# First element of a graph network kernel: another order of its loads, biases as rows, y plus x on VectorE

## The chip, the cores and the metric

The kernel runs on one core of a Trainium2 chip. The metric is the device time of one execution in microseconds (us), a median over runs. A profiled execution gives the trace; its times are us from the start of its span unless marked ns. The engines are PE (TensorE, matmuls; PEld are its weight loads), DVE (VectorE), ACT (ScalarE), POOL (GpSimd) and SP (SyncE, which here only issues DMA transfers). ACT and POOL can issue transfers too.

## The reference

`x` is (16, 1024, 128), `adj` is (16, 1024, 1024), all in float32. A first graph layer is followed by a network of four layers with skip connections; each adds its input and normalises:

```python
# layer 0
degree = adj.sum(-1)[:, :, None]
agg = einsum('bid,bij->bjd', x, adj) / degree
x1 = layernorm(x + relu(concat([x, agg], -1) @ W.T + b))
# layer 1: four layers with inputs of 128, 128, 256 and 384 features
def layer(nodes, adj, ws, bs, wd, bd, wn, bn, wu, bu):
    src_agg = einsum('bjv,bij->biv', nodes @ ws + bs, l2norm(adj, 2))   # rows scaled
    dst_agg = einsum('bjv,bji->biv', nodes @ wd + bd, l2norm(adj, 1))   # columns scaled
    return tanh(concat([src_agg, nodes @ wn + bn, dst_agg], 2) @ wu + bu)
out = layernorm(x1 + four_layers(x1, adj))
```

## The kernel before

The 16 elements of the batch are worked off one after the other, and an element's preparation (loads, squares, norms, first graph layer) lies beside the products of the element before it. Element 0 has nothing before it, so its preparation is written out by hand ahead of the loop. The order on every engine is the order in which the program issues the instructions; pools of buffers and semaphores add waits, but nothing is reordered.

**Blocks.** `adj[0]` (4.2 MB) is held in the tile `a` as 8 blocks of 128 rows by 1024 columns. Two blocks are a row pair, and `PAIRS` lists the four pairs: the two of the second half of the nodes (h = 1) first, then those of h = 0. Each pair comes as four pieces, one for each group `g` of 32 partitions, each 256 KB. `x[0]` (0.5 MB) comes as four pieces of 64 KB a half into `xn`.

**Loads before.** SP issues `w0n` (the first layer's weights), then groups 0 and 1 of x of both halves, then groups 0 and 1 of all four row pairs. POOL issues the groups 2 and 3 of each. SP goes on with `b0c`, and then by layers with the weights and the four biases (`fetch_weights`; a bias is a column, one element of 4 bytes in each of 128 partitions), with row blocks of `adj` in another arrangement (`load_rows`, eight pieces of 128 KB for each of four quarters q) after layers 1, 2 and 3. The completions of SP's transfers use eight semaphores in turn, so a transfer is issued only when the eighth before it has landed. In the trace this is an SP issue that waits for a DMA.

**First graph layer.** `to_xT` transposes x on TensorE, with a copy on ACT. `weights_of_x` multiplies it by half of W into `pw`. `with_x` (L1168) multiplies the identity by x into a bank `pn`, to which y is added later. For each pair `squares_of` takes the squares of its two blocks with their sums on ACT (L1119) and the row sums (degrees) on VectorE (L1125), and `gathers_of` multiplies x by the blocks into `pa` (L1132, 128x512 each; a matmul in float32 shows as two instructions). `degree_inverses` and `degree_row` make 1/degree a row, by a reciprocal on VectorE, a transpose on TensorE (`dinv`, L359) and a copy on ACT. In block `second` = 3 the degree is taken on ACT (L1199). `scaled` is `pa` times that row (`agT`), `weights_of_agT` the second half of W, with the relu on ACT (`yT`, L1163). `with_y` (L1174) adds y to `pn` by products of yT with the identity. `norm_stats` takes mean and variance on VectorE, `norm_write_act` (ACT, L490) and `norm_write` (VectorE, L486) write x1 to `x1n`, and `to_x1` transposes it.

**Folding of weights.** A layer's ws, wd and wn are multiplied by wu ahead of use: `fold_begin` transposes them on TensorE (L205), copies them out (L206), and multiplies the biases by wu (L209, L211); `fold_end` multiplies the weights (L227) and copies them (L229, L230). Layers 0 and 1 are folded beside the normalisation. The folds of layers 2 and 3 stand in the loop over the products of layer 0 (`plain_layer`): before step i of its list of matmuls it calls `hooks[i]`, 5 and 8 for layer 2, 9 and 12 for layer 3. `small` hands out TensorE banks of a pool of two, `product` those of a pool of four.

**Layer 0 of element 0.** `messages` makes the messages in four groups of blocks, in the order 2, 3, 0, 1 (L247, `pt`), and calls `between[n]` after group n. After the third comes `row_factors0`: the inverse row norms are spread (L381), summed over groups on TensorE (`rp`, L252), copied (`rinv`), and two quarters of rows are scaled by them on ACT (L647). `plain_layer` then does the own products z, the destination products d (L851), and the source products z with the transposed rows (`at`, from VectorE's transposes, L655).

Of the kernel before, what the change touches and what calls it, by code (L numbers as in the profile page):

```python
# [8 lines left out]
F32 = mybir.dt.float32  # L9
# [14 lines left out]
def adj_resnorm_kernel(ctx: ExitStack, tc: tile.TileContext, x, adj, w0, b0, layers, out):  # L24
# [147 lines left out]
    def message_tile(name):  # L172

        return one.tile([P, max(WIDTH)], F32, tag="wm", name=name)
# [2 lines left out]

        return wm if l in PAIRED else wm[:, :KEPT[l] * 2 * P].rearrange("p (c v) -> p c v", v=2 * P)

    def fetch_weights(raw, l, q, wm=None):  # L180
        ws, bs, wd, bd, wn, bn, wu, bu = layers[l]
        nch = CHUNKS[l]
        size = max(3 * nch * P, KEPT[l] * 2 * P, WIDTH[l])
        flat = raw.take(size) if wm is None else wm[:, WIDTH[l]:]
        wr = flat[:, :3 * nch * P].rearrange("p (k c v) -> p k c v", k=3, c=nch)
        for k, w in enumerate((ws, wd, wn)):
            q.dma_start(wr[:, k], w.rearrange("(c p) v -> p c v", p=P))
        wur = raw.take(3 * P).rearrange("p (k v) -> p k v", k=3)
        q.dma_start(wur, wu.rearrange("(c p) v -> p c v", p=P))
        bc = raw.take(4)  # L190
        for k, v in enumerate((bs, bd, bn, bu)):
            q.dma_start(bc[:, k:k + 1], v.rearrange("(p o) -> p o", o=1))
# [48 lines left out]
    def small(name, shape=(K,)):  # L241
        return ps_s.tile([P, *shape], F32, tag="small", name=name)
# [811 lines left out]
    def load_pair(q, pair, groups):  # L1054
        h, k = pair
# [3 lines left out]
    def load_nodes(q, h, groups):  # L1059
        for g in groups:  # L1060
            q.dma_start(xn[g * C:(g + 1) * C, h * BPH:(h + 1) * BPH], xv[h][g])

    nc.sync.dma_start(w0n, w0)
    shares = ((nc.sync, range(G // 2)), (nc.gpsimd, range(G // 2, G)))
    for h in (1, 0):
        for q, groups in shares:
            load_nodes(q, h, groups)
    make_identity(nc, ident)
    for pair in PAIRS:
        for q, groups in shares:  # L1070
            load_pair(q, pair, groups)
    nc.sync.dma_start(b0c, b0.rearrange("(p o) -> p o", o=1))
    raw = Raw()
    wm = message_tile("wm1_0")
    Q = combined(0, "Q")
    places = {q: Q[i].rearrange("p k (u c) -> p (k u) c", u=2) for q, i in ((2, 2), (3, 3), (0, 4))}
    places[1] = one.tile([P, 2 * NJ, HW // 2], F32, tag="T2", name="rows1_0")
    rows, fetched = {}, []
    for l, q in enumerate((None, 2, 3, None)):
        fetched.append(fetch_weights(raw, l, nc.sync, None if l else wm))  # L1080
        if q is not None:
            rows[q] = load_rows(0, q, [places[q]])
    wm = as_chunks(wm, 0)
# [18 lines left out]
    pt = small("w0tr", [HW])  # L1102
    for k in range(2):
        nc.tensor.transpose(pt[:, k * P:(k + 1) * P], w0n[:, k * P:(k + 1) * P], ident)
    nc.scalar.copy(w0T.rearrange("p k v -> p (k v)"), pt[:, :2 * P])

    sq = []
    for p in (3, 4):
# [12 lines left out]
    def add_square(i):  # L1121
        nc.gpsimd.tensor_add(sq[4], sq[4], sq[i])
# [41 lines left out]

    def with_x(h):

        pn[h] = ps_t.tile([P, BPH, P], F32, tag="pt", name=f"yn0_{h}")
        nc.tensor.matmul(pn[h].rearrange("p q d -> p (q d)"), ident, xn[:, h * BPH:(h + 1) * BPH].rearrange("p q d -> p (q d)"),  # L1168
                         start=True, stop=False)

    def with_y(h):
        for q in range(BPH):
            i = h * BPH + q
            nc.tensor.matmul(pn[h][:, q], yT[:, i * P:(i + 1) * P], ident, start=False, stop=q == BPH - 1)  # L1174

    def to_x1(h):
        pt = product(f"x1tr_{h}")
# [8 lines left out]
    for pair in PAIRS[:2]:  # L1186
        squares_of(*pair)
        gathers_of(*pair)
    nc.vector.tensor_add(sq[6], sq[6], sq[7])
    add_square(5)  # L1190
    add_square(6)
# [26 lines left out]
    fold_end(0, fetched[0])  # L1218
    stats[0] = norm_stats(pn[0], range(BPH), "0_0_0")
    root_inverses(cols, inv, slice(NB))  # L1220
    add_square(second)
    biases = fold_begin(1, fetched[1], nc.vector.tensor_copy, True)
    for q in range(BPH):
        norm_write_act(x1n[:, BPH + q], pn[1][:, q], stats[1], q)
    to_x1(1)
    biases()
    fold_end(1, fetched[1])
    for q in range(BPH):
        norm_write(x1n[:, q], pn[0][:, q], stats[0], q)


    kept = scratch.tile([N, D], F32, tag="kept", name="kept0")
# [9 lines left out]
    for b in range(B):  # L1242
# [7 lines left out]
        f1 = feature(b, "f1T")  # L1250
        if b == 0:
            def row_factors0():
                nonlocal rinv
                rinv = gather_inverses(0, row_inverses(0, inv))
                column_sums(0, st0)
                for q in (2, 3):
                    scale_rows(rows[q], q, rinv)

            t = messages(b, 0, feats, wm, {0: lambda: to_x1(0), 2: row_factors0}, with_sums=False)
            cinv = {}  # L1260

            def columns0(rows, h, engine=nc.vector):
# [2 lines left out]
            def rows0(destination, finish):  # L1265
                for q in (2, 3):
                    transpose_rows(rows[q], q, at)

            def cinv0(destination, finish):
                cinv[0] = factor_rows_now(0, 1, inv, "cinv")  # L1270

            def second0(destination, finish):
                columns0(range(NJ, NB), 1)
                sums_of_weights(2, fetched[2][3])
                weight_sums(own_seven(2, fetched[2][3]))
                nc.sync.dma_start(wsave[2], fetched[2][3])
                destination(1, cinv[0])
                columns0(range(NJ), 1)

# [380 lines left out]
```

## Time and profile before

| what | value |
|---|---|
| median of 3 runs | 2398.15 us (2396.02 to 2398.34) |
| the profiled execution | 2396.57 us |
| its span in the trace | 2394.8 us |
| PE busy | 2377.7 us, 99% |
| first instruction of the gathers | 13.31 us |
| first source product z of layer 0 | 67.64 us |
| DMA, 0 to 60 us | 12.37 MB, mean 206 GB/s |

The span is what the trace shows; 1.77 us lie around it. A row of an engine gives the start, the busy time, the line, what is written from what, and in brackets the idle time before it with its cause. The ends of matmuls are modelled, so rows of PE overlap a little. Everything that the change touches lies ahead of 67.64 us.

### The profile page before, as it was taken

How to read it: one execution, taken by the hardware profiler on the slowest of the kernel's cores; microseconds unless marked ns; L12 is line 12 of the kernel's file. 1: busy time of each engine (PE TensorE's matmuls, PEld its weight loads, DVE VectorE, ACT ScalarE, POOL GpSimd, SP SyncE). 2: the span in 40 equal slices, each digit the busy share in tenths (PEclk: the TensorE clock that was granted, in tenths of full speed). 3: DMA queues.
4: the chain of work that ended last, by engine and by line, in shares of the span. 5: the costliest groups of instructions: out<-in, count | busy, mean ns of one | idle time of the engine just before them, and what ended most of it. 6: DMA issues, size and time to landing. Idle time of an engine off the chain costs nothing.

```text
span 2394.8 us, 39324 instructions
## 1 busy us (share of the span) xinstructions
PE 2377.7 (99%) x15293; PEld 1288.4 (54%) x15293; DVE 2089.2 (87%) x2814; ACT 980.3 (41%) x1842; POOL 273.8 (11%) x102
## 2 busy tenths in 40 slices
PE   8999999999999999999999999999999999999998
PEld 4444554645556455554655546455464555645555
DVE  5998888999889989889988889888899888998954
ACT  5524345253343524435244452534525344352322
POOL 4101111001111011110111110111100111101110
PEclk9999999999999999999999999999999999999999
DMA  9527244262633627335272442634426253362400
GB/s 206 123 75 146 69 114 90 70 148 57 137 75 81 138 48 157 61 97 116 55 163 56 107 97 71 147 69 111 91 69 151 57 132 78 80 141 48 100 22 22
DMA packets 365897, 232.03 MB, mean 97 GB/s; under 512 B 152784, under 2 KB 336848, under 8 KB 365712
## 3 DMA queue, kind: packets, MB, share of 16 engines
q1 hardware_dynamic: 364944, 227.16, 42.6%
q0 software_dynamic: 768, 2.36, 0.4%
q8 instruction: 121, 1.98, 0.4%
q14 instruction: 64, 0.52, 0.1%
HBM read 209.59 MB, written 19.84 MB: 96 GB/s over the span
## 4 chain that ended last, share of the span: by engine, by line
PE 95%; DVE 2%; DMA 1%; SPq 1%; issue 1%; ACT 0%; POOLq 0%; DVEq 0%
PE m L1005 40%; PE z L1005 29%; PE pt L247 9%; PE pt_z L247 5%; PE m_f L583 5%; PE z_f L583 2%; PE pw L247 2%; PE m3s L1005 1%; PE z L851 1%; DMA wm<-in_L_gnn_ws_dram 1%; PE pt_p L247 1%; SPq L640 1%; DVE acc L331 0%; DMA a<-in_adj_dram 0%; PE d L851 0%
## 5 line engine op out<-in xcount | busy, mean ns | idle before, releaser
L1005 PE MATMUL m<-a,t 128*64 128x512 f32 x1008 | 434.6, 593 | 0.2 <-DVE t L711 0.2
L1005 PE MATMUL m<-at,t 128*64 128x512 f32 x1008 | 418.5, 592 | 0.0
L1005 PE MATMUL m<-Q,S 128*64 128x512 f32 x880 | 394.0, 593 | 0.0
L1005 PE MATMUL m<-T,S 128*64 128x512 f32 (+1 forms) x1040 | 393.5, 573 | 0.0
L456 POOL TENSOR_TENSOR rs<-ve,mhalf 128x32 f32<-128x32 f32 x30 | 191.9, 6396 | 987.9 <-DVE ve L454 987.9
L1005 PE MATMUL z<-at,t 128*64 128x512 f32 x504 | 229.2, 592 | 0.0
L1005 PE MATMUL z<-at,S 128*64 128x512 f32 x504 | 228.3, 593 | 0.0
L1005 PE MATMUL z<-a,S 128*64 128x512 f32 x504 | 228.2, 593 | 0.0
L1005 PE MATMUL z<-a,t 128*64 128x512 f32 x504 | 227.2, 593 | 0.0
L1005 PE MATMUL z<-Q,t 128*64 128x512 f32 x504 | 227.0, 593 | 0.0
L1005 PEld LDWEIGHTS m<-T,S 128*64 128x64 f32 x1040 | 131.0, 137 | 128.5 <-issue 126.5
L1005 PEld LDWEIGHTS m<-Q,S 128*64 128x64 f32 x880 | 118.2, 137 | 147.9 <-issue 141.0
L1005 PEld LDWEIGHTS m<-a,t 128*64 128x64 f32 x1008 | 131.9, 137 | 108.7 <-issue 100.0
L1005 PEld LDWEIGHTS m<-at,t 128*64 128x64 f32 x1008 | 131.3, 137 | 109.4 <-issue 108.0
L1005 PE MATMUL z<-T,t 128*64 128x512 f32 x384 | 172.8, 592 | 0.0
L884 ACT COPY e<-m 64x512 f32<-64x512 f32 x63 | 36.6, 582 | 327.9 <-PE m L1005 327.5
L376 POOL TENSOR_TENSOR inv<-cols,mhalf 128x16 f32<-128x16 f32 (+1 forms) x17 | 46.8, 2752 | 1031.2 <-DVE cols L375 1031.2
L414 DVE TENSOR_TENSOR a<-a,cinv 128x512 f32<-128x512 f32 x250 | 154.1, 694 | 1.9 <-ACT cinv L351 1.3
L322 ACT ACTIVATE sq<-a 128x1024 f32<-128x1024 f32 x120 | 125.9, 1050 | 37.1 <-DVE acc L329 23.2
L247 PE MATMUL pt<-wm,f1T 128*64 128x128 f32 (+1 forms) x1536 | 133.8, 309 | 0.0
L247 PEld LDWEIGHTS pt<-wm,f1T 128*64 128x64 f32 x1536 | 110.3, 137 | 31.9 <-issue 12.3
L317 ACT ACTIVATE a<-a 128x1024 f32<-128x1024 f32 x120 | 125.3, 1045 | 0.4
(302 smaller groups left out, 5019.8 us busy)
## 6 DMA issues: line engine op xcount, KB each, us to landing
a<-in_adj_dram SPq DMA_DIRECT2D x120, 512.0 KB, 12.3
rows<-in_adj_dram SPq DMA_DIRECT2D x480, 64.0 KB, 2.1
a<-in_adj_dram SPq DMA_DIRECT2D x240, 128.0 KB, 3.5
wm<-wsave SPq DMA_DIRECT2D x32, 704.0 KB, 5.0
wm<-wsave SPq DMA_DIRECT2D x31, 320.0 KB, 3.2
xn<-in_x_dram SPq DMA_DIRECT2D x124, 64.0 KB, 5.5
xs<-in_x_dram SPq DMA_DIRECT2D x60, 128.0 KB, 3.6
cinv<-dr SPq DMA_DIRECT2D x30, 256.0 KB, 6.4
```

The source lines that it names most:

```text
L247: nc.tensor.matmul(out[s], x[:, s], y, start=start, stop=stop)
L317: nc.scalar.activation(a[:, i, :], a[:, i, :], AF.Copy, accum_out=degree)
L322: nc.scalar.activation(sq, a[:, i, :], AF.Square, accum_out=state["cols"][:, i:i + 1])
L376: nc.gpsimd.tensor_tensor(inv[:, s], cols[:, s], mhalf[:, s], ALU.pow)
L414: engine.tensor_mul(a[:, i, s], a[:, i, s], cinv[:, s])
L456: nc.gpsimd.tensor_tensor(rstd, ve, mhalf[:, :n], ALU.pow)
L583: nc.tensor.matmul(o, x_, y_, start=start, stop=stop)
L640: nc.sync.dma_start(piece[g * C:(g + 1) * C, :, h * P:(h + 1) * P], v[h, g, :, k:k + n])
L851: nc.tensor.matmul(nodes(o) if len(y.shape) == 4 else o, x_, y, start=start, stop=stop)
L884: nc.scalar.copy(e0[high], A[high])
L1005: nc.tensor.matmul(o, x, y_, start=start, stop=stop)
```

## The change

- **Loads.** x of half 1 goes first on SP, w0 and x of half 0 on ACT. Of pairs 0 and 1 SP loads three groups and POOL the fourth; pairs 2 and 3 are loaded by POOL alone. x and `w0n` are no longer on POOL or ahead of x on SP.
- **Biases.** Each bias is loaded as a row of 128 elements into one partition of a tile, b0 and those of layers 0 and 1 before the weights, those of layers 2 and 3 after the weights of layer 1. `bias_columns` turns them to columns by one transpose on TensorE and a copy on ACT (and one more for `b0c`).
- **Order of SP's later loads.** Weights of layers 0, 1, 2, row quarter 2, weights of layer 3, row quarters 3, 0 and 1.
- **Zero products.** TensorE begins with two 128x512 products of a tile of zeros, which nobody reads.
- **Order on TensorE at the start.** Both halves of x are transposed, then w0, then the two products of x.
- **y plus x.** `with_x` now transposes y into a bank and VectorE adds x from `xn`, into `x1n`, which the normalisation then reads and overwrites. The products by the identity, of x and of y, are gone. The square of block `second` comes after yT of half 0 on ACT.
- **Fold of layer 2.** It moves from hooks 5 and 8 to the messages, after groups 2 and 3; the spread of the row norms goes with it, and `rp` follows the fold's end. The sums of layer 2's weights on VectorE move from hook 11 to hook 6.

```diff
@@ fetch_weights: the four bias loads are gone, bc is handed in @@
-        bc = raw.take(4)
-        for k, v in enumerate((bs, bd, bn, bu)):
-            q.dma_start(bc[:, k:k + 1], v.rearrange("(p o) -> p o", o=1))
@@ loads of element 0 @@
-    nc.sync.dma_start(w0n, w0)
-    shares = ((nc.sync, range(G // 2)), (nc.gpsimd, range(G // 2, G)))
-    for h in (1, 0):
-        for q, groups in shares:
-            load_nodes(q, h, groups)
+    idle = one.tile([P, HW], F32, tag="S2", name="idle")
+    nc.vector.memset(idle, 0.0)
     make_identity(nc, ident)
-    for pair in PAIRS:
-        for q, groups in shares:
-            load_pair(q, pair, groups)
-    nc.sync.dma_start(b0c, b0.rearrange("(p o) -> p o", o=1))
+    load_nodes(nc.sync, 1)
+    nc.scalar.dma_start(w0n, w0)
+    load_nodes(nc.scalar, 0)
+    load_pair(nc.sync, 0, (0, 1, 2))
+    load_pair(nc.gpsimd, 0, (3,))
+    load_pair(nc.gpsimd, 1, (3,))
+    load_pair(nc.sync, 1, (0, 1, 2))
+    load_pair(nc.gpsimd, 2, range(G))
+    load_pair(nc.gpsimd, 3, range(G))
...
+    def load_biases(i):
+        for k, v in enumerate(biases_of[i]):
+            nc.sync.dma_start(in_rows[k:k + 1, i * P:(i + 1) * P], v.rearrange("(o p) -> o p", o=1))
+
+    def bias_columns(i):
+        n = len(biases_of[i])
+        pt = small(f"biases{i}")
+        nc.tensor.transpose(pt[:, :n], in_rows[:n, i * P:(i + 1) * P], ident[:n, :n])
+        nc.scalar.copy(columns[i], pt[:, :n])
+        if i == 0:
+            nc.scalar.copy(b0c, pt[:, :1])
+
+    load_biases(0)
...
-    for l, q in enumerate((None, 2, 3, None)):
-        fetched.append(fetch_weights(raw, l, nc.sync, None if l else wm))
+    for l, q in enumerate((None, None, 2, 3)):
+        if l == 2:
+            load_biases(1)
+        fetched.append(fetch_weights(raw, l, nc.sync, bcs[l], None if l else wm))
...
+    pt = product("idle")
+    for _ in range(2):
+        nc.tensor.matmul(pt, idle[:, :P], idle, start=True, stop=True)
...
     def with_x(h):
-        pn[h] = ps_t.tile([P, BPH, P], F32, tag="pt", name=f"yn0_{h}")
-        nc.tensor.matmul(pn[h]..., ident, xn[:, h * BPH:(h + 1) * BPH]..., start=True, stop=False)
-
-    def with_y(h):
+        pt = ps_t.tile([P, BPH, P], F32, tag="pt", name=f"yn0_{h}")
         for q in range(BPH):
             i = h * BPH + q
-            nc.tensor.matmul(pn[h][:, q], yT[:, i * P:(i + 1) * P], ident, start=False, stop=q == BPH - 1)
+            nc.tensor.transpose(pt[:, q], yT[:, i * P:(i + 1) * P], ident)
+        pn[h] = x1n[:, h * BPH:(h + 1) * BPH]
+        nc.vector.tensor_add(pn[h], pt, xn[:, h * BPH:(h + 1) * BPH])
@@ order of the first graph layer @@
-    for h in (1, 0):
-        to_xT(h)
-        with_x(h)
-        weights_of_x(h)
+    to_xT(1)
+    to_xT(0)
+    transposes_of_w0()
+    weights_of_x(1)
+    weights_of_x(0)
...
     gathers_of(*PAIRS[2])
+    bias_columns(0)
...
     square(first)
-    square(second)
     gather(0, second)
     add_square(first)
-    with_y(1)
     scaled(0)
+    with_x(1)
     weights_of_agT(0)
     stats = {1: norm_stats(pn[1], range(BPH), "0_0_1", True)}
+    square(second)
     fold_begin(0, fetched[0])
-    with_y(0)
+    with_x(0)
@@ layer 0 of element 0 @@
             def row_factors0():
-                nonlocal rinv
-                rinv = gather_inverses(0, row_inverses(0, inv))
                 column_sums(0, st0)
                 for q in (2, 3):
                     scale_rows(rows[q], q, rinv)
...
+            def second_x1():
+                to_x1(0)
+                bias_columns(1)
+                fold_begin(2, fetched[2])
+                ahead["spread"] = row_inverses(0, inv)
+
+            def factors_and_fold():
+                nonlocal rinv
+                fold_end(2, fetched[2])
+                rinv = gather_inverses(0, ahead["spread"])
...
-            t = messages(b, 0, feats, wm, {0: lambda: to_x1(0), 2: row_factors0}, with_sums=False)
+            t = messages(b, 0, feats, wm, {0: second_x1, 1: factors_and_fold, 2: row_factors0}, with_sums=False)
...
-            hooks = {4: lambda *_: inverses(0, st0, NB), 5: folded(2, fold_begin), 6: rows0, 7: cinv0,
-                     8: folded(2, fold_end), 9: lambda *_: fold_and_scale(3, 0), 11: second0, 12: folded(3, fold_end),
+            hooks = {4: lambda *_: inverses(0, st0, NB), 6: rows0, 7: cinv0,
+                     9: lambda *_: fold_and_scale(3, 0), 11: second0, 12: folded(3, fold_end),
```

More of the change, by code (lines that the diff above doesn't have):

```diff
@@ L178, in as_chunks, with fetch_weights @@
         return wm if l in PAIRED else wm[:, :KEPT[l] * 2 * P].rearrange("p (c v) -> p c v", v=2 * P)
-    def fetch_weights(raw, l, q, wm=None):
+    def fetch_weights(raw, l, q, bc, wm=None):
         ws, bs, wd, bd, wn, bn, wu, bu = layers[l]
@@ L1052, in adj_resnorm_kernel, with load_pair, load_nodes @@
     PAIRS = [(h, k) for h in (1, 0) for k in range(0, BPH, 2)]
-    def load_pair(q, pair, groups):
-        h, k = pair
+    def load_pair(q, i, groups):
+        h, k = PAIRS[i]
         for g in groups:
             q.dma_start(a[g * C:(g + 1) * C, h * BPH + k:h * BPH + k + 2], av[h][g, :, k:k + 2])
-    def load_nodes(q, h, groups):
-        for g in groups:
+    def load_nodes(q, h):
+        for g in range(G):
             q.dma_start(xn[g * C:(g + 1) * C, h * BPH:(h + 1) * BPH], xv[h][g])
-    nc.sync.dma_start(w0n, w0)
-    shares = ((nc.sync, range(G // 2)), (nc.gpsimd, range(G // 2, G)))
-    for h in (1, 0):
-        for q, groups in shares:
-            load_nodes(q, h, groups)
-    make_identity(nc, ident)
-    for pair in PAIRS:
-        for q, groups in shares:
-            load_pair(q, pair, groups)
-    nc.sync.dma_start(b0c, b0.rearrange("(p o) -> p o", o=1))
-    raw = Raw()
+    idle = one.tile([P, HW], F32, tag="S2", name="idle")
+    nc.vector.memset(idle, 0.0)
+    make_identity(nc, ident)
+    load_nodes(nc.sync, 1)
[7 more added lines that the diff above has]
+    load_pair(nc.gpsimd, 3, range(G))
+    biases_of = [[b0, *layers[0][1::2], *layers[1][1::2]], [*layers[2][1::2], *layers[3][1::2]]]
+    in_rows = one.tile([P, HW], F32, tag="S3", name="biases")
+    raw = Raw()
+    columns = [raw.take(len(v)) for v in biases_of]
+    bcs = [columns[0][:, 1:5], columns[0][:, 5:], columns[1][:, :4], columns[1][:, 4:]]
+    def load_biases(i):
[9 more added lines that the diff above has]
+    load_biases(0)
     wm = message_tile("wm1_0")
@@ L1100, in to_xT, with transposes_of_w0 @@
         nc.scalar.copy(nodes(xT[:, half(h)]), blocks(pt))
[L1102 to L1105, printed above, removed]
+    pt = product("idle")
+    for _ in range(2):
+        nc.tensor.matmul(pt, idle[:, :P], idle, start=True, stop=True)
+    def transposes_of_w0():
+        pt = small("w0tr", [HW])
+        for k in range(2):
+            nc.tensor.transpose(pt[:, k * P:(k + 1) * P], w0n[:, k * P:(k + 1) * P], ident)
+        nc.scalar.copy(w0T.rearrange("p k v -> p (k v)"), pt[:, :2 * P])
     sq = []
@@ L1165, in with_x @@
     def with_x(h):
-        pn[h] = ps_t.tile([P, BPH, P], F32, tag="pt", name=f"yn0_{h}")
-        nc.tensor.matmul(pn[h].rearrange("p q d -> p (q d)"), ident, xn[:, h * BPH:(h + 1) * BPH].rearrange("p q d -> p (q d)"),
-                         start=True, stop=False)
-    def with_y(h):
+        pt = ps_t.tile([P, BPH, P], F32, tag="pt", name=f"yn0_{h}")
         for q in range(BPH):
             i = h * BPH + q
-            nc.tensor.matmul(pn[h][:, q], yT[:, i * P:(i + 1) * P], ident, start=False, stop=q == BPH - 1)
+            nc.tensor.transpose(pt[:, q], yT[:, i * P:(i + 1) * P], ident)
+        pn[h] = x1n[:, h * BPH:(h + 1) * BPH]
+        nc.vector.tensor_add(pn[h], pt, xn[:, h * BPH:(h + 1) * BPH])
     def to_x1(h):
@@ L1180, in to_x1 @@
         nc.scalar.copy(x1T[:, half(h)], pt)
-    for h in (1, 0):
-        to_xT(h)
-        with_x(h)
-        weights_of_x(h)
-    for pair in PAIRS[:2]:
-        squares_of(*pair)
-        gathers_of(*pair)
+    to_xT(1)
[3 more added lines that the diff above has]
+    weights_of_x(0)
+    squares_of(*PAIRS[0])
+    gathers_of(*PAIRS[0])
+    squares_of(*PAIRS[1])
+    gathers_of(*PAIRS[1])
     nc.vector.tensor_add(sq[6], sq[6], sq[7])
@@ L1223, in adj_resnorm_kernel @@
     for q in range(BPH):
-        norm_write_act(x1n[:, BPH + q], pn[1][:, q], stats[1], q)
+        norm_write_act(pn[1][:, q], pn[1][:, q], stats[1], q)
     to_x1(1)
@@ L1228, in adj_resnorm_kernel @@
     for q in range(BPH):
-        norm_write(x1n[:, q], pn[0][:, q], stats[0], q)
+        norm_write(pn[0][:, q], pn[0][:, q], stats[0], q)
     kept = scratch.tile([N, D], F32, tag="kept", name="kept0")
@@ L1257, in row_factors0 @@
                     scale_rows(rows[q], q, rinv)
-            t = messages(b, 0, feats, wm, {0: lambda: to_x1(0), 2: row_factors0}, with_sums=False)
+            def second_x1():
[7 more added lines that the diff above has]
+                rinv = gather_inverses(0, ahead["spread"])
+            ahead = {}
+            t = messages(b, 0, feats, wm, {0: second_x1, 1: factors_and_fold, 2: row_factors0}, with_sums=False)
             cinv = {}
@@ L1267, in rows0 @@
                     transpose_rows(rows[q], q, at)
+                sums_of_weights(2, fetched[2][3])
+                weight_sums(own_seven(2, fetched[2][3]))
+                nc.sync.dma_start(wsave[2], fetched[2][3])
             def cinv0(destination, finish):
@@ L1273, in second0 @@
                 columns0(range(NJ, NB), 1)
-                sums_of_weights(2, fetched[2][3])
-                weight_sums(own_seven(2, fetched[2][3]))
-                nc.sync.dma_start(wsave[2], fetched[2][3])
                 destination(1, cinv[0])
```

## The prediction

> **What bounds the kernel now.** I read the page's busy times first, then the busy time by stretches of the span, then TensorE's order of time in the first 68 us, and last the chain of waits and SP's own waits.
>
> ```profile
> PE 2377.7 (99%) x15293; PEld 1288.4 (54%) x15293; DVE 2089.2 (87%) x2814; ACT 980.3 (41%) x1842; POOL 273.8 (11%) x102
> ```
>
> By stretches (from and to, length, busy us of PE, its weight loads, DVE, ACT and POOL with their instructions, granted clock, DMA share, GB/s):
>
> ```profile
> 0.00:13.30 13.30, 7.81 (x18) 3.79 (x19) 0.83 (x5) 2.83 (x5) 7.36 (x19) 1.00 0.83 222
> 13.30:20.40 7.10, 7.09 (x16) 2.85 (x16) 5.94 (x7) 4.37 (x8) 2.39 (x2) 1.00 1.05 267
> ...
> 294.00:440.00 146.00, 146.00 (x952) 79.39 (x950) 131.32 (x176) 61.29 (x114) 15.68 (x4) 1.00 0.43 98
> ```
>
> TensorE is busy 2377.7 of 2394.8 us, so 17.1 us are idle in the whole span; an inner element (294 to 440) has none. The change touches only element 0, up to about 67.6 us, where the z products start. From there on the order is the old one, so what is won or lost before 67.6 shifts the rest. Nothing after it is freed: DVE's backlog begins at an addition that waits for z (1.7 us at 73.0 to 74.7) and moves with TensorE, and the two later stalls (1.2 and 1.0 us, on the differences of layer 2's features) move with it. TensorE in order of time (start, busy, line, what, count, and in brackets the idle time before it with its cause):
>
> ```profile
> 13.31 7.11 PE L1132 MATMUL pa<-a,xn 128*128 128x512 f32 x16 [1.10 <-issue]
> 20.45 0.62 PE L359 MATMUL dinv<-ident,inv 128*128 128x128 f32 x4
> ...
> 41.31 0.31 PE L252 MATMUL rp<-sp,fold 128*64 128x32 f32 x4 [0.89 <-DVE sp L381]
> ...
> 48.80 0.71 PE L209 MATMUL bm<-raw 128*128 128x128 f32 x4 [0.70 <-ACT raw L206]
> ```
>
> And from the waits (us, times, longest):
>
> ```profile
> DVE cols L1125 <- DMA a<-in_adj_dram: 8.2, 1, 8.2
> ```
>
> The gathers start at 13.31, when the first row pair is complete (VectorE waited 8.2 us for it). From there to 67.6 TensorE has 54.3 us, of which the rows with a gap, 0.89 + 0.70 + 0.30 + 0.24 + 0.20 us and some tenths at the second pair, are all that is idle. So element 0 is a wait for data, then a nearly full TensorE. From the chain of waits (start, length, what), and the order of time on DVE and ACT:
>
> ```profile
> 9.29 13.66 DMA wm<-in_L_gnn_ws_dram
> ```
>
> ```profile
> 24.85 0.18 DVE L1129 RECIPROCAL inv<-cols 128x4 f32<-128x4 f32 x1 [0.84 <-ACT sq L1199]
> ...
> 31.26 0.69 ACT L1163 ACTIVATE yT<-pw,b0c 128x512 f32<-128x512 f32 x1
> ...
> 31.84 0.47 ACT L206 COPY raw<-wtr 128x384 f32<-128x384 f32 x1
> ```
>
> The first line says that a 64 KB weight lay 13.7 us behind the row pairs; SP issues a transfer only when the eighth before it has landed, so its queue crept until 22.97 us. The landings of SP's eight row transfers can be read from these waits: 8.19, 9.29, 10.23, 12.23, 13.94, 15.65, 17.38, 19.64.
>
> **What the Trainium skill says.** "DMA: Bandwidth & Descriptors", section "Issuing engines are not separate DMA queues": queues of several engines run on the same 16 DMA engines and save only issue time. The trace agrees: 303 to 311 GB/s with two queues full, and SP's pieces of 262 kB then land every 1.71 us, which is 153 GB/s, half. Its section "Queues, rings and completion order" says that an engine goes round robin between queues, hence the half. "TensorE: Matmul & The Clock Gate", Part 1: the clock is at half rate until some 3.4 us of activity. The trace agrees in durations: the first 128x512 halves took 0.83 us in the mean, later ones 0.59, though PEclk shows 1.00.
>
> **The change, part by part.** All against the profiled execution: 2396.57 us, of which 2394.8 span and 1.77 around it. That is 1.58 below the median of the three runs, 2398.15; I put the sum on the median.
>
> 1. *Loads.* Pair 0 and pair 1 now have three pieces (0.79 MB) on SP and one on POOL; pairs 2 and 3 are eight POOL pieces. SP's first piece waits for x to land (issue 0.74 + a landing of 2.0 to 4.4, so about 3.8; before, 3.09). The x pieces also share with POOL's rows, which start near 2 us as POOL has no x to issue. x complete near 5.1 (TensorE's first transpose of x was at 5.07), then 0.79 MB at 153 GB/s is 5.2 us: pair 0 at 10.5 (bounds 9.5 and 12.5), pair 1 at 15.6 (14.0 and 17.0). Before: 13.28 and 16.72. Gathers of one pair are 8 instructions at 0.43 = 3.5 us, so those of pair 0 end at 14.0 and TensorE then waits for pair 1. Of the 2.8 us by which pair 0 is earlier, 1.1 is left: **-1.1** (-2.7 to +0.3).
> 2. *Zero products, x alone first, products of x.* Four product instructions ident times xn go (4 at 0.83 = 3.3 us), four of zeros come. Both lie ahead of the first pair, and before there was a gap of 1.10 us. Now TensorE must be through by 10.5: x of half 0 at about 6.3 (its last piece on ACT's queue waits for one of half 1), transposes 1.0, copies of xT and w0T 0.6 + 0.4, products 1.7 warm or 3.6 cold: 10 to 12. Warmed it just fits; cold it eats into step 1 but not past pair 1, which decides. 0 (0 to +0.5). Five issues on ACT ahead of its table load (5 at 0.43, then 1.28) end near 5.2, when the first copy is due: 0.
> 3. *Bias rows.* 17 column loads become 17 row loads: the same issues of about 0.45 us on SP. But with six row pieces instead of eight on SP, the queue is free by about 16 instead of 22.97, and 56 issues at 0.48 later it has the last rows at 43 to 45 instead of 53.4. No TensorE gap before was put down to these rows: 0. New is work on ACT: two copies out of the bias transposes (about 0.25 each, as the 128x128 copy of 0.27), which cannot start until TensorE has done pair 2's gathers (24.4 in old times). ACT's next, the degree of the second row (L1199, 23.68), starts then at 25.2 and ends 26.4 instead of 24.8; VectorE's reciprocal waits for it and TensorE's dinv transposes for that: 26.6 instead of 26.06. **+0.5** (0 to +1.0). The same place is hit if pair 3, now all on POOL's queue, is late: that queue moves 2.62 MB instead of 2.36 and finished at 22.7; in proportion it ends at 22.5 to 25, where 24 is needed. Upper end +2.0 in all.
> 4. *y plus x.* The y products (8 instructions, 1.16 us a half) become four transposes (0.6), so TensorE has 0.56 less per half; VectorE has one addition more per half (128x512 from PSUM, 0.69, as agT). On the path agT, statistics, x1n, these give +0.1. At the same place square(second), 1.04 + 0.19, moves on ACT behind yT of half 0. That yT waits for TensorE (31.2) whatever stands ahead, so nothing is won; the wtr copy behind it moves from 31.84 to 33.1. The copies of wm (33.86) and the four x1n writes (34.29) follow it by 0.7 to 0.8, and x1tr and the messages follow those. **+0.7** (0 to +1.4).
> 5. *Fold of layer 2* moves from the products d (hooks 5 and 8) into the messages. Its work is the same. Gone are the 0.89 before rp (covered now by its six wm products) and the 0.70 at bm (ACT was then scaling rows, 6.49 us; now the fold is ahead of it). New is its own round trip: x1T copy 0.59, bias copy 0.25, before the second transposes, about 0.5. **-1.1** (-1.6 to +0.5). ACT's scaling starts 2 to 3 us later; z needs it (by DVE's transposes) only at 66, and they end by 54. If that cover were gone it would cost its 2 to 3 us. The nine weight sums (2.3 us, DVE) move ahead of the column scaling, where DVE waited 1.3 for cinv: 0.
>
> Sum: -1.1 + 0 + 0.5 + 0.7 - 1.1 = -1.0. 2398.15 - 1.0 = **2397.1 us**.
>
> **The rivals.** First, *all gains arrive*: POOL's queue gets less than half, pair 1 lands at 14 or earlier, and ACT has room for its copies: -2.7 + 0 + 0.1 - 1.6, about -4.2, so 2394. For it: in 8.2 to 10.2 us SP's pieces landed every 1.0 us. Against: POOL had just begun to move then. To pass 0.2% (4.8 us, about what a measurement of this kernel can tell from no change) it needs yet another 0.6.
> Second, *POOL's queue is the bound*: pairs 2 and 3 come from one queue that is behind two others and the weights. The point from which it decides is a landing of pair 3 after 24; at half rate throughout (17 us for 2.62 MB from 5) it is 22, but if three queues (ACT's x, SP, POOL) leave it a third early and SP's weights later, 26 to 30: +2 to +6, with the rest at -1 that is 2399 to 2403. Against: the weights are issued at 64 KB per 0.45 us, 145 GB/s, so no more than half. Slower than before, and past 0.2% only at its far end.
> Third, *nothing moves*: x lands late under POOL's large pieces, pair 1 stays at 16.7, the fold's round trip eats its gap: 2398.
>
> **How the numbers follow.** Likeliest case (net -3 to +1) 0.66, all gains 0.14, POOL's queue late 0.10, nothing moves 0.10. Range 2393.5 to 2401.0: the sum's -1.0 with the bounds of steps 1, 3 and 5, and 1 us for the median. Within 0.2% is 2393.35 to 2402.95: faster 0.08 (half of "all gains" and a little), same 0.87, slower 0.05 (half of "POOL late").
>
> **What would show it.** Right: pa starts near 10.5 with a gap of 1 to 2 us after its first 8 instructions; SP's weights are issued by 16 to 18 us; the degree activation starts only after the bias copies; the wtr copy of layer 0 comes 1 us later after yT than before; no gap before rp; z starts near 66.6 instead of 67.64. Wrong: pa starts at 13 or later, a gap of over 1 us between pair 2 and 3, z's start over 2 us away from 66.6, or differences after z.

## The result, and the profile after

The changed kernel takes **2405.12 us** in the median of 7 runs (2403.3 to 2405.57), against 2398.15 (2395.93 to 2398.34) for 7 runs of the kernel before beside it: a ratio of 1.0031, 95% interval 1.0019 to 1.0043 (a ratio is worked out from all single executions; the two medians alone give 1.0029). One execution of e9 below took 9160.29 us and is left out of its ratio. The kernel is slower by 0.31% and outside the predicted range, on the side to which the prediction gave a chance of 0.05. The profiled execution is the one of 2405.12 us, span 2403.3, against 2396.57 and 2394.8. The single runs of the kernel before stand in part near 2396 and in part near 2398; in the four larger sets taken later (19 to 41 runs each) its median was 2396.10 to 2396.47. Against those the loss is 9 us, and the two traces show about the same (8.5 us by their spans).

Line by line against those shown of before. The busy times:

```profile
PE 2381.0 (99%) x15287; PEld 1282.9 (53%) x15287; DVE 2090.9 (87%) x2817; ACT 980.7 (41%) x1845; POOL 273.4 (11%) x100
```

TensorE is busy for 3.3 us more with six instructions fewer, and idle for 22.3 us instead of 17.1. The two together are the 8.5 us by which the span is longer. The busy part is mostly matmuls at half speed, as the order of time will show. The same stretches as before (length, busy us of PE, weight loads, DVE, ACT, POOL, granted clock, DMA share, GB/s):

```profile
0.00:13.30 13.30, 4.87 (x8) 1.89 (x8) 1.17 (x5) 1.87 (x2) 6.27 (x17) 1.00 0.85 201
13.30:20.40 7.10, 4.08 (x9) 2.32 (x10) 2.34 (x2) 2.94 (x6) 0.43 (x1) 1.00 1.04 220
294.00:440.00 146.00, 146.00 (x953) 78.91 (x951) 131.39 (x175) 60.96 (x114) 15.68 (x4) 1.00 0.44 98
```

The inner element is full as before. In the first 20.4 us less arrived: 13.3 us at 201 and 7.1 at 220 GB/s are 4.2 MB, where before 222 and 267 GB/s made 4.8 MB (the products of the rates and times, rounded). The DMA share is no lower, so the engines were occupied and moved less. TensorE in order of time:

```profile
1.46 3.78 PE L1123 MATMUL idle<-idle 128*128 128x512 f32 x4 [1.46 <-DVE mhalf L1106]
9.38 1.08 PE L1118 MATMUL xtr<-ident,xn 128*128 128x128 f32 x4 [4.14 <-DMA xn<-in_x_dram]
15.79 1.11 PE L1118 MATMUL xtr<-ident,xn 128*128 128x128 f32 x4 [5.33 <-DMA xn<-in_x_dram]
16.70 0.63 PE L1128 MATMUL w0tr<-ident,w0n 128*128 128x128 f32 x2
17.86 3.78 PE L1183 MATMUL pw<-x_T,w0T 128*128 128x512 f32 x4 [0.52 <-ACT w0T L1129]
21.43 8.33 PE L1156 MATMUL pa<-a,xn 128*128 128x512 f32 x16
29.60 0.60 PE L356 MATMUL dinv<-ident,inv 128*128 128x128 f32 x4
...
42.89 0.94 PE L224 MATMUL wm<-raw 128*128 128x128 f32 x6 [0.75 <-ACT raw L203]
...
53.20 0.31 PE L249 MATMUL rp<-sp,fold 128*64 128x32 f32 x4
...
76.76 3.60 PE L848 MATMUL z<-at,t 128*128 128x512 f32 x8
```

Of before, the transposes of the second half of x and the first z:

```profile
9.39 1.02 PE L1099 MATMUL xtr<-ident,xn 128*128 128x128 f32 x4
...
67.64 12.61 PE L851 MATMUL z<-at,t 128*128 128x512 f32 x29
```

TensorE waits for x twice, 4.14 and 5.33 us, and transposes the second half at 15.79 where the kernel before had it at 9.39. The gathers start at 21.43 instead of 13.31 and z at 76.76 instead of 67.64: **9.1 us** late, of which 8.1 arise ahead of the first gather. The `rp` products have no gap any more, as foretold. From z to the end of the span it is 2326.5 us here and 2327.2 before; in the other kernels below it is 2326.1 to 2327.2, so nothing after z differs by more than this scatter. The chain of waits (start, length, what) begins:

```profile
0.74 2.87 DMA w0n<-in_L_gnn_W_dram
...
3.62 12.12 DMA xn<-in_x_dram
...
15.79 1.13 PE xtr L1118 x4
```

Before, the chain ran through a weight behind row pairs; now it is one 64 KB piece of x on ACT's queue that took 12.12 us. And the waits of VectorE and of SP's own queue (us in total, times, longest):

```profile
DVE cols L1149 <- DMA a<-in_adj_dram: 19.7, 2, 14.6
```

```profile
SPq L1080 <- DMA a<-in_adj_dram: 6.7, 3, 2.4
SPq L1080 <- DMA xn<-in_x_dram: 5.5, 1, 5.5
...
SPq L1054 <- DMA xn<-in_x_dram: 4.4, 4, 2.4
```

SP's row issues (L1054) and its second bias (L1080) wait for pieces of x. SP in order of time shows how far that pushes them:

```profile
0.74 1.81 SPq L1058 DMA_DIRECT2D xn<-in_x_dram  x4
3.37 6.49 SPq L1054 DMA_DIRECT2D a<-in_adj_dram  x6
9.90 0.34 SPq L1080 DMA_DIRECT2D biases<-in_L_gnn_b_dram  x1
15.77 0.22 SPq L1080 DMA_DIRECT2D biases<-in_L_gnn_bs_dram  x1
...
24.66 0.36 SPq L187 DMA_DIRECT2D wm<-in_L_gnn_ws_dram  x1
```

The six row pieces go out between 3.37 and 9.86, and the second bias at 15.77, when the last x piece of *ACT* had landed: ACT's transfers take their turn in the same eight semaphores as SP's. Meanwhile POOL had issued its first eight row pieces:

```profile
1.50 4.40 POOL L1054 DMA_DIRECT2D a<-in_adj_dram  x8 [0.18 <-issue]
```

Before, POOL had its x first:

```profile
4.25 4.20 POOL L1057 DMA_DIRECT2D a<-in_adj_dram  x8
```

So POOL's rows began at 1.50 instead of 4.25. Two of the eight belong to pairs 0 and 1, the rest to pairs 2 and 3.

### The profile page after: what moved, and what is told of

Read it like the earlier page. It is cut to its first block, busy times and chain, and to the rows that moved or that the text cites. A ratio compares the mean times of both kernels' runs of the same rounds, so it can differ in the third digit from the quotient of the medians.

```text
span 2403.3 us, 39330 instructions
## 1 busy us (share of the span) xinstructions
PE 2381.0 (99%) x15287; PEld 1282.9 (53%) x15287; DVE 2090.9 (87%) x2817; ACT 980.7 (41%) x1845; POOL 273.4 (11%) x100
## 3 DMA queue, kind: packets, MB, share of 16 engines
q0 software_dynamic: 800, 2.62, 0.5%
q8 instruction: 121, 1.98, 0.4%
## 4 chain that ended last, share of the span: by engine, by line
PE 96%; DVE 2%; ACT 1%; DMA 1%; issue 0%; POOLq 0%; DVEq 0%; ACTq 0%
PE m L1002 40%; PE z L1002 28%; PE pt L244 9%; PE pt_z L244 5%; PE m_f L580 5%; PE z_f L580 2%; PE pw L244 2%; PE z L848 1%; PE pa L1156 1%; PE m3s L1002 1%; PE pt_p L244 1%; DMA xn<-in_x_dram 1%; PE d L848 0%; DVE acc L328 0%; ACT a L314 0%
```

## The experiments

All times are us; "x half 0" is the start of its transposes (which TensorE can reach late: where the data had landed clearly earlier, that time, from the semaphore events of the trace, stands in brackets), "pair" the start of the row sums on it, "gathers" the first `pa`, z the first source product. Ratios are to runs of the kernel before on the same chip.

| kernel | x half 0 | pair 0 / pair 1 | gathers | z | ratio, 95% interval |
|---|---|---|---|---|---|
| before | 9.39 (7.52) | 13.30 / 16.7 | 13.31 | 67.64 | |
| after | 15.79 | 16.70 / 24.20 | 21.43 | 76.76 | 1.0031, 1.0019 to 1.0043 |
| e1_loads_alone | 15.30 | 16.29 / 22.95 | 17.56 | 73.84 | 1.0031, 1.0019 to 1.0043 |
| e2_old_loads | 8.14 | 13.37 / 16.65 | 13.75 | 68.35 | 1.0000, 0.9991 to 1.0009 |
| e3_old_x_new_pairs | 7.98 | 11.54 / 16.24 | 13.59 | 68.03 | 0.9999, 0.9991 to 1.0008 |
| e4_new_x_old_pairs | 14.72 | 14.38 / 17.89 | 20.14 | 74.16 | 1.0029, 1.0018 to 1.0039 |
| e5_pool_held | 7.91 | 14.74 / under 17 | 14.76 | 69.13 | 1.0009, 1.0001 to 1.0017 |
| e6_x0_on_pool | 8.86 | 11.91 / 15.71 | 14.47 | 69.08 | 1.0000, 0.9991 to 1.0008 |
| e7_clock_held | 7.37 | 11.25 / 15.53 | 11.27 | 67.05 | 0.9998, 0.9990 to 1.0007 |
| e8_best | 8.38 | 12.23 / 18.16 | 12.25 | 69.87 | 0.9995, 0.9987 to 1.0003 |
| e9_x0_long_runs | 7.62, with half 1 (5.01) | 14.56 / 20.40 | 14.57 | 71.29 | 1.0016, 1.0009 to 1.0022 |
| e10_x0_late_in_order | 28.06 (15.43) | 17.00 / 24.54 | 17.01 | 77.45 | 1.0038, 1.0024 to 1.0052 |
| e11_fold_alone | 8.38 | 13.30 / 16.60 | 13.32 | 67.97 | 0.9995, 0.9987 to 1.0003 |
| e12_x0_four_long | 12.42 | 16.26 / 23.77 | 18.07 | 74.66 | 1.0031, 1.0019 to 1.0043 |

### Which part of the change: e1_loads_alone and e2_old_loads

e1 is the kernel before with only the loads of w0, x and the pairs from the changed one; e2 is the reverse.

```diff
@@ e1, against before @@
+    load_nodes(nc.sync, 1)
+    nc.scalar.dma_start(w0n, w0)
+    load_nodes(nc.scalar, 0)
+    load_pair(nc.sync, 0, (0, 1, 2))
+    load_pair(nc.gpsimd, 0, (3,))
...
@@ e2, against after @@
+    nc.sync.dma_start(w0n, w0)
+    for h in (1, 0):
+        for q, groups in shares:
+            load_nodes(q, h, groups)
...
+    for i in range(len(PAIRS)):
+        for q, groups in shares:
+            load_pair(q, i, groups)
```

> The kernel before with only the new loads of w0, x and the row pairs (x on SP and ACT, three groups of pairs 0 and 1 on SP, pairs 2 and 3 on POOL); biases as columns and all orders as before. Theory L (the loads carry the loss: x of half 0 on ACT's queue lands near 15.8 us because POOL's rows are already on the DMA engines, and pair 1 near 24 because pairs 2 and 3 compete with it): gathers start at 20 or later, z of layer 0 starts at 77 to 78.5 (9 to 11 later than 67.64; the fold's gain is missing), time +7.5 to +10 against before. Rival O (the other parts carry it: cold clock, bias rows, y plus x on VectorE, order on ACT): at most +3, z at 71 or earlier.

> The changed kernel with the loads of w0, x and row pairs as they were before (halves on SP and POOL, x and w0 first); everything else as changed. Theory L: the loss is gone, gathers start near 13, z of layer 0 at 66.5 to 67.5, time -1.5 to 0 against before. Rival O: +4 or more against before, z at 72 or later.

e1 took 2404.0 us against 2396.15, 7.9 more; e2 took 2396.73, 0.6 more, with 1 inside its interval. The loads alone carry the loss, and without them it is gone. Biases, y plus x, zero products and fold together cost e2 0.7 us at z, where a gain had been expected.

Both expectations missed z. The profiled execution of e1, the fastest of its six (2402.05), has z at 73.84, 6.2 late and not 9 to 11. There the gathers start 2.26 us after the transposes of x half 0 (15.30 to 17.56), in the changed kernel 5.64 us after (15.79 to 21.43). The old order had the products of half 1 done while it waited; the new one has w0 and all four products, at half speed, behind the late half. So the new order on TensorE adds to the loss once x is late.

### Which part of the loads: e3_old_x_new_pairs and e4_new_x_old_pairs

```diff
@@ e3, against after: only w0 and x loaded as before @@
-    load_nodes(nc.sync, 1)
-    nc.scalar.dma_start(w0n, w0)
-    load_nodes(nc.scalar, 0)
+    nc.sync.dma_start(w0n, w0)
+    for h in (1, 0):
+        for q, groups in shares:
+            load_nodes(q, h, groups)
@@ e4, against after: only the pairs loaded as before @@
-    load_pair(nc.sync, 0, (0, 1, 2))
...
+    for i in range(len(PAIRS)):
+        for q, groups in shares:
+            load_pair(q, i, groups)
```

> The changed kernel with w0 and x loaded as before (groups 0 and 1 on SP, 2 and 3 on POOL, ahead of the rows), the row pairs three to one as changed. Tells the two halves of theory L apart. If x behind POOL's rows is all of it: x lands by 9, pair 0 near 11 to 12, z at 67 to 68, time -1 to +1. If the pairs on POOL's queue (2 and 3 competing with pair 1) are all of it: pair 1 still lands near 20 to 24 and the gathers of pair 1 wait for it, z at 72 to 76, time +5 to +7. I expect a split: pair 1 at 19 to 20, z near 70, time +2 to +4.

> The changed kernel with x on SP and ACT as changed, but all row pairs in halves over SP and POOL as before. If x on ACT's queue behind POOL's rows is the cause: x of half 0 still lands after 12, gathers start at 17 or later, time +4 to +6. If only the pairs' split matters: x lands by 7, gathers at 12 to 13, time -1 to +1. I expect x late, gathers at 16 to 19, then no wait at pair 1, time +3 to +5.

e3 took 2396.12 against 2396.15, e4 2402.96. So it is where x is issued, not the split of the pairs, and not the share of both that was expected of e3. (What the split adds once x is late is not shown: z is at 74.16 in e4 and 76.76 in the changed kernel, but the ratios 1.0029 and 1.0031 don't tell the two apart.) With x loaded as before, the three-to-one pairs landed much as predicted. VectorE of e3 in order of time:

```profile
11.54 2.35 DVE L1151 TENSOR_REDUCE cols<-a 128x1 f32<-128x1024 f32 x2 [6.44 <-DMA a<-in_adj_dram]
16.24 2.35 DVE L1151 TENSOR_REDUCE cols<-a 128x1 f32<-128x1024 f32 x2 [2.35 <-DMA a<-in_adj_dram]
```

But TensorE could not take pair 0 at 11.54, as its own list in e3 shows:

```profile
7.98 1.08 PE L1120 MATMUL xtr<-ident,xn 128*128 128x128 f32 x4 [1.89 <-DMA xn<-in_x_dram]
...
10.02 3.78 PE L1185 MATMUL pw<-x_T,w0T 128*128 128x512 f32 x4 [0.52 <-ACT w0T L1131]
13.59 7.44 PE L1158 MATMUL pa<-a,xn 128*128 128x512 f32 x16
```

The products of x ran at half speed until 13.6, which step 2 of the prediction had set at zero because pair 1 would decide. And even with the old loads TensorE waits for x half 0 until 7.98.

### Why x is late: e5_pool_held and e6_x0_on_pool

e5 makes POOL read a column of each half of x before it issues rows; e6 puts x half 0 on POOL ahead of its rows (and of the identity matrix that POOL makes), so its rows begin at 4.26.

```diff
@@ e5, against after @@
+    hold = one.tile([P, 2], F32, tag="hold", name="hold")
+    for h in range(NH):
+        nc.gpsimd.tensor_copy(hold[:, h:h + 1], xn[:, h * BPH, :1])
     load_pair(nc.sync, 0, (0, 1, 2))
@@ e6, against after @@
+    load_nodes(nc.sync, 1)
+    load_nodes(nc.gpsimd, 0)
+    nc.scalar.dma_start(w0n, w0)
     make_identity(nc, ident)
-    load_nodes(nc.sync, 1)
-    nc.scalar.dma_start(w0n, w0)
-    load_nodes(nc.scalar, 0)
```

> The changed kernel, x on SP and ACT as changed, but POOL issues its row pieces only after x has landed (two copies of one column of xn on POOL stand ahead of them). Theory A1 (the x pieces are late because POOL's rows are already being moved by the same DMA engines): x complete by 5 to 6.5 us, gathers from 13 to 15, z of layer 0 at 68 to 70, time +0.5 to +2.5 against before. Theory A2 (ACT's queue, or a third queue, is slow for these pieces whatever else runs): x of half 0 lands after 9 as before the hold, z at 72 or later, +4 or more.

> The changed kernel with one thing moved: x of half 0 is issued by POOL, ahead of its row pieces, not by ACT (w0 stays on ACT, x of half 1 on SP). A1: both halves land by 6, gathers from 12.5 to 14, z at 67.3 to 68.5, time -1 to +1. If SP's half is delayed by POOL's rows all the same (they follow x closely): half 1 at 7 to 9, gathers near 15, z near 69.5, time +1.5 to +2.5.

POOL of e5, and TensorE of e5, in order of time:

```profile
7.92 0.34 POOL L1068 COPY hold<-xn 128x1 f32<-128x1 f32 x2 [6.60 <-DMA xn<-in_x_dram]
8.68 4.41 POOL L1054 DMA_DIRECT2D a<-in_adj_dram  x8 [0.42 <-issue]
```

```profile
5.40 1.07 PE L1121 MATMUL xtr<-ident,xn 128*128 128x128 f32 x4 [0.16 <-DMA xn<-in_x_dram]
7.91 0.66 PE L1121 MATMUL xtr<-ident,xn 128*128 128x128 f32 x4 [1.44 <-DMA xn<-in_x_dram]
```

x half 0 is there at 7.91 instead of 15.79, from the same ACT queue and with the same pieces; the only difference ahead of it is that POOL's rows are not under way. SP's own rows are, even earlier than in the changed kernel (out at 3.18 to 6.28), so they are not the cause. Half 1 on SP gains as well, 5.40 instead of 9.38. e6, with POOL's rows behind x, has half 0 at 8.86 and half 1 at 5.99; its z (69.08) lies between the two cases of its expectation, its time (+0.75 us by the medians) in the first. So x is late because POOL's row pieces are under way with it or ahead of it on the same engines. e5 gives 2 us of the gain away again (2398.11 against 2396.10), as its pair 0 needs a piece of POOL's that is issued only at 8.68.

### What makes x lose: e9_x0_long_runs and e12_x0_four_long

A piece of x comes in runs of 512 bytes. Both kernels give each partition four consecutive nodes and so 2 KB in one run, e9 in one transfer, e12 in four as in the changed kernel. The nodes of this half then stand in another order than their rows of `adj`, so the result of element 0 is not the reference's; the amount of work is the same.

```diff
@@ e9, against after @@
-    load_nodes(nc.scalar, 0)
+    nc.scalar.dma_start(xn[:, :BPH].rearrange("p k d -> p (k d)"),
+                        x[0, half(0)].rearrange("(p k) d -> p (k d)", p=P))
@@ e12, against after @@
-    load_nodes(nc.scalar, 0)
+    xr = x[0, half(0)].rearrange("(p k) d -> p (k d)", p=P)
+    for g in range(G):
+        nc.scalar.dma_start(xn[g * C:(g + 1) * C, :BPH].rearrange("p k d -> p (k d)"), xr[g * C:(g + 1) * C])
```

> The changed kernel with x of half 0 on ACT's queue as one transfer of 128 runs of 2 KB instead of four with 512 runs of 512 B; same bytes, same queue, POOL's rows (4 KB runs) as changed. The nodes of that half stand in another order then, so element 0's result is another one; the amount of work is the same. Theory P (queues get turns on an engine by packets, so a queue of small packets gets few bytes): x of half 0 lands by 7 to 9 instead of 15.8, TensorE starts the gathers only when the first pair is there, near 16 if the rows stay as late; time +3 to +6 against before. Theory B (turns by bytes, or the queue is slow): x of half 0 lands at 14 or later, time as the changed kernel's, +8 to +9.

> As the run with one transfer of long runs, but x of half 0 still comes as four transfers of 64 KB on ACT's queue, each of 32 runs of 2 KB instead of 128 of 512 B: only the length of the runs is changed (the nodes of that half of element 0 again stand in another order, so its result is another one). If the length of the runs was what let the half land at 7.5 us: again 7 to 8.5, time +3 to +5 against before. If the number of transfers and the wait of the last of them for a half 1 piece did it: 11 or later, time +6 to +9.

The DMA queues of the first 30 us (packets, MB, share of 16 engines), first after, then e12, where q0 is POOL's queue and q10 ACT's:

```profile
q0 software_dynamic: 800, 2.62, 39.3%
...
q10 hardware_dynamic: 720, 0.39, 5.3%
```

```profile
q10 hardware_dynamic: 336, 0.39, 5.2%
```

A packet is 3.3 KB on POOL's queue (2.62 MB over 800) and 0.55 KB on ACT's, which has w0 beside x; 1.2 KB in e12. The Trainium skill, "DMA: Bandwidth & Descriptors", section "Queues, rings and completion order", says that an engine goes round robin between queues packet by packet. If those packets are the ones counted here, a turn of POOL's carries six times the bytes of a turn of x, and the half that the prediction took from this section fits only queues whose packets are alike. The direction agrees: longer runs brought x half 0 from 15.79 to 12.42 in e12, outside the 14.72 to 15.79 of e4, e1 and the changed kernel.

That is the smaller part. e9, with nearly e12's packets (288), had x half 0 landed at 5.01; its TensorE starts only at 7.62 because half 1 is later there (7.49). e12 came out on the second branch of its expectation, but the wait of its fourth piece is not for half 1, as the expectation and the prediction have it: the fourth takes over the semaphore of `w0n`, landed at 3.60 in the changed kernel, and goes out at 3.62. The four pieces landed at 4.03, 7.87, 9.52 and 15.75 in the changed kernel and at 4.39, 5.71, 6.99 and 12.37 in e12 (semaphore events of the traces), so the last one alone costs 5 to 6 us in both. In e5 it goes out as late (3.53), and had landed by 7.86: the late issue costs this much only with POOL's rows under way. Between e9 and e12 are thus the number of transfers, their spread over partitions (128 at once against 32 each) and the late fourth. Which of them counts was not separated.

SP's own queue in e9 shows the second consequence:

```profile
2.59 3.38 SPq L1054 DMA_DIRECT2D a<-in_adj_dram  x6
```

With three fewer transfers in the turn of eight, SP had its six rows out at 5.97 instead of 9.86, 3.9 us earlier, and pair 1 landed at 20.40 instead of 24.20, 3.8 earlier. In e3, with rows out at 6.09 but POOL's rows begun at 4.25 instead of 1.50, it landed at 16.24. So two delays of pair 1 can be read: SP's issues held by x, and POOL's head start with pairs that are needed last. The second is argued from two kernels that also differ in the loads of x.

### Could another order on TensorE hide it: e10_x0_late_in_order

```diff
@@ e10, against after @@
-    to_xT(0)
...
-    weights_of_x(0)
...
     gathers_of(*PAIRS[0])
     squares_of(*PAIRS[1])
     gathers_of(*PAIRS[1])
+    to_xT(0)
+    weights_of_x(0)
```

> The changed kernel with all its loads; only TensorE's order is another: the transposes and the product of x of half 0 stand behind the gathers of pairs 0 and 1, which don't need it. Tells how much of the loss is TensorE's order behind the late x and how much the late rows. If the order is nearly all: gathers start as pair 0 lands (16 to 17), pair 1's at its landing, the dinv transposes at 22 to 24 instead of 29.6, time +2 to +4. If the rows of pair 1 (landing 24.1) are late whatever TensorE does: dinv at 28 to 29, z at 75 to 76, time +7 to +8. I expect the second.

It took 2406.09 against 2396.47, as slow as the changed kernel, and past even the expected +7 to +8. TensorE in order of time:

```profile
17.01 5.33 PE L1156 MATMUL pa<-a,xn 128*128 128x512 f32 x8 [4.04 <-DMA a<-in_adj_dram]
24.55 3.67 PE L1156 MATMUL pa<-a,xn 128*128 128x512 f32 x8 [2.21 <-DMA a<-in_adj_dram]
...
30.30 0.60 PE L356 MATMUL dinv<-ident,inv 128*128 128x128 f32 x4
```

TensorE no longer waits for x half 0, and now waits for pair 1 until 24.55. The late x and the late pair 1 lie side by side: to take TensorE's wait away and leave x's hold on SP's queue gains nothing. e12 says the same from the other side: its x came 3.4 us earlier, its pair 1 still at 23.77, and it stayed 7.4 us slower than the kernel before (2403.6 against 2396.17).

### What the other steps are worth: e7_clock_held, e8_best, e11_fold_alone

e7 is e3 with one more zero product between the transposes of the two halves of x. e8 is e7 with the bias columns moved behind the degree of `second` on ACT and the square of `second` back ahead of yT of half 0. e11 is the kernel before with only the fold of layer 2 moved (and with it the spread of the row norms and the sums of that layer's weights).

```diff
@@ e7, against e3 @@
+    def zeros(n):
...
     to_xT(1)
+    zeros(1)
     to_xT(0)
@@ e8, against e7 @@
-    bias_columns(0)
...
@@ behind the degree of second @@
+    bias_columns(0)
@@ behind square(first) @@
+    square(second)
@@ behind yT of half 0 @@
-    square(second)
@@ e11, against before @@
-            t = messages(b, 0, feats, wm, {0: lambda: to_x1(0), 2: row_factors0}, with_sums=False)
+            t = messages(b, 0, feats, wm, {0: second_x1, 1: factors_and_fold, 2: row_factors0}, with_sums=False)
...
```

> The kernel of the third run (old x, new pairs) with one zero product more, between the transposes of the two halves of x, where TensorE waited 1.9 us for data. If the products of x ran at half speed (3.78 us for four) because that wait let the clock fall: they take 1.9 to 2.2, the gathers start near 11.8 instead of 13.59, pair 1 (16.2) then decides, z at 67.5 to 67.7 instead of 68.03, time -0.6 to 0 against the third run. If the clock is not the cause: 3.8 again, gathers at 13.6.

> The kernel of the run before this one, with the two costs on ACT taken back as well: the bias transposes and copies stand behind the degree on ACT (step 3 put 0.5 us on them), and square(second) ahead of yT of half 0 as before the change (step 4 put 0.7 us on it). If these steps were sized right, z at 66.2 to 67.0 and time -0.8 to -2 against before; if they cost nothing, z as in the run before this one, 67.5.

> The kernel before with only the fold of layer 2 (and the spread of the row norms, and the sums of its weights) moved into the messages, all loads and orders as before. Step 5 of the prediction put 1.1 us on this. If that is right: z of layer 0 at 66.3 to 66.9 instead of 67.64, no gap before rp, time -0.5 to -1.5 against before. If the gain came only with the other parts: z at 67.4 or later, no difference.

e7: TensorE in order of time.

```profile
5.54 1.02 PE L1127 MATMUL idle<-idle 128*128 128x512 f32 x2
7.37 0.63 PE L1120 MATMUL xtr<-ident,xn 128*128 128x128 f32 x4 [0.81 <-issue]
...
8.95 1.98 PE L1189 MATMUL pw<-x_T,w0T 128*128 128x512 f32 x4 [0.73 <-ACT w0T L1135]
11.27 3.70 PE L1162 MATMUL pa<-a,xn 128*128 128x512 f32 x8 [0.34 <-DMA a<-in_adj_dram]
```

The same four products take 1.98 us instead of 3.78, pair 0 is taken as it lands, and z comes at 67.05, 1.0 earlier than in e3 and 0.6 earlier than before. Not all of the 1.0 is the clock's: pair 1 happened to land 0.7 earlier than in e3 (15.53 against 16.24), and TensorE waits for it. What the zero product is worth at z lies between 0.3 and 1.0.

e8 took 2395.01 in the median, 1.1 us under the kernel before. In its profiled execution pair 1 landed at 18.16, 2.6 later than in e7 from the same loads, so its z says little. What can be read is the stretch that it changed: from the second `dinv` to the transposes of x1 it is 8.71 us, 9.59 in e2, e3, e7 and after, and 9.09 before.

e11 took 2395.34 against 2396.17. From the first messages to z it is 29.62 us, before 30.77: the fold gives **1.15**. Its gathers took 8.80 us instead of 7.11, in part at half speed after an idle stretch of 2.53; 1.5 of that is still there at the messages, and after the fold 0.3 at z (67.97 against 67.64). So z came later than expected in this one execution, 1.7 us above the median of its kernel.

The intervals of e7, e8 and e11 include 1, so none of them is shown to beat the kernel before; by the medians they are 0.6 to 1.1 us below it.

## Why the prediction was wrong, point by point

**Step 1, loads: this is the step that failed**, at "x complete near 5.1". x was complete at 15.75, 10.6 us later (9.4 by the "about 6.3" that step 2 has for half 0). Two things were wrong in it.

The smaller is a reading. "TensorE's first transpose of x was at 5.07" is a transpose of half 1 alone. Half 0 was complete at 7.52 in that same trace, where TensorE came to it only at 9.39; e3 and e2, with these loads, wait for it until 7.98 and 8.14. So 2 to 3 us of the 10.6 were there before the change.

The larger, about 8 us, is the share. The prediction had named the cause ("share with POOL's rows, which start near 2 us") and the third rival even said "x lands late under POOL's large pieces", but both put its cost at nothing. e5 and e6 show that POOL's early rows are the cause. The rest of the step, "pair 0 at 10.5" and "pair 1 at 15.6", holds within its bounds when x is loaded as before (11.54 and 16.24 in e3).

The failure had a second half in the sentence "SP's first piece waits for x to land (... about 3.8)". It waited until 3.37, but the following pieces waited too, since the turn of eight semaphores takes in ACT's five transfers; the last row left SP at 9.86. "The queue is free by about 16" became 24.66 for the first weight (17.00 in e3, as predicted).

**Step 2, zero products: 0 to +0.5.** The text weighed "1.7 warm or 3.6 cold" and let pair 1 cover the cold case. Measured 3.78, so cold. In e2 the gathers start 0.44 later than before, within the bounds. Where pair 0 does come early, "not past pair 1" fails: in e3 pair 1 at 16.24 and its gathers of 3.67 would end at 19.9, and the first `dinv` is at 20.87. That is why e3, the kernel nearest to what the prediction describes, does not show the -1.1 of step 1: its z is 0.4 later than before. e7, with the four products at full speed, is 0.6 earlier.

**Step 3, bias rows: +0.5.** Between the two `dinv` transposes e2 has 5.95 us and before 5.61: +0.34. The chain is as described: the degree (L1224) starts at 33.98, after the copies at 33.83 and 33.90. But TensorE shows no wait for it; 0.15 of the 0.34 is the bias transpose itself. In e8, with the columns moved, it is 5.84.

**Step 4, y plus x: +0.7.** From the second `dinv` to x1tr +0.50 (9.59 against 9.09). That "the wtr copy of layer 0 comes 1 us later after yT" was right: 1.63 us from the start of yT to that copy, 0.58 before, and TensorE waits 0.75 for it at `wm`. In e8, with the square back, the stretch is 0.88 shorter than with it moved, and 0.38 shorter than before. That would make y plus x on VectorE itself a gain of about 0.4; it is read from one trace, of a kernel that also has its bias columns elsewhere.

**Step 5, fold: -1.1.** -1.15 in e11, -1.0 in the changed kernel (+10.12 us at the first messages, +9.12 at z). This step was right in size and reason: the two gaps of 0.89 and 0.70 before `rp` and `bm` became one of 0.40 at `bm` in e11.

So steps 3, 4 and 5 were within their bounds, step 2 only where pair 0 is late, and step 1 was off by 8 us ahead of the first gather. Of the rivals, "POOL's queue is the bound" put the wait at pair 3, where the trace shows none; what was late is the transfer in front of it. "Nothing moves" had the right mechanism and gave it no cost. The sum was also put on a median of 2398.15 that larger sets place near 2396.2.

**Open.** Why the DMA engines moved fewer bytes at the same busy share (220 against 267 GB/s) was not tested by itself; nor was why the fourth piece of x, out at 3.62, took 12.12 us while the third, out at 2.14, took 7.4.

## What to carry to other kernels

Before a small transfer that everything waits for is put on a queue of its own, look at what other queues issue in the same microseconds: here the queue freed of x began its 256 KB pieces 2.75 us earlier, and the 64 KB pieces of x landed some 8 us later than where they stood ahead of the rows on both queues (15.79 against 7.98 in e3). Price such a transfer by the bytes under way beside it and by when its last piece can be issued, not by an equal share per queue, and count who reuses its completion semaphore. Look up the landing of each piece, not the first instruction that reads one of them. A queue that loads what is needed last had better start last: with POOL's rows from about 4.25, pair 1 came at 16.24 (e3) and 15.71 (e6); with rows from 1.51 and SP not held by x, at 20.40 (e9).

## What the runs showed of the hardware that was not expected

- TensorE can fall to half speed, for part of the next products, after waits of little over 2 us. Gathers of one pair took 3.67 us after waits of 2.17 (e9) and 2.21 us (e10), but 5.37 after 2.23 (e8) and 5.33 after 4.04 (e10); two pairs took 8.80 after 2.53 (e11), 7.11 before. The profile's granted clock shows this in one case and not in the other: 0.72 in e8 from 18 to 24, 1.00 in e10 from 17 to 22.4; the durations show it in both. The Trainium skill, "TensorE: Matmul & The Clock Gate", Part 1, has half rate after an idle window of about 3.4 us that runs freely; here slow gathers followed a wait of 2.23 us. TensorE in e8:

```profile
18.18 5.37 PE L1162 MATMUL pa<-a,xn 128*128 128x512 f32 x8 [2.23 <-DMA a<-in_adj_dram]
```

- The same loads land at different times from one kernel to the next: pair 1 at 16.24, 15.53 and 18.16 in e3, e7 and e8. A difference of 1 or 2 us in one trace is no effect until a second one shows it.
- Issuing a bias as a row mostly takes SP 0.22 to 0.25 us in the changed kernel, as a column 0.33 to 0.48 before.
